# Both slots' maxima on VectorE in one go, the first slot's transposed half after them: a change of order in an attention loop

## The chip, the cores and the metric

The kernel runs on one core of one Trainium2 chip. The metric is the device time of one execution in microseconds; the time before is the median of three runs. The kernel is written in Bass with Tile, in float32 throughout.

## The reference, cut to what matters

The whole program has four layers on x of shape (2, 256, 64, 64): attention, an added position term, a bottleneck with a deformable 3x3 convolution, and a block of two deformable 3x3 convolutions with group norms. The change is in the first layer:

```python
xn = group_norm(x, gn_gamma, gn_beta)                       # 8 groups
qkv = einsum('bchw,oc->bohw', xn, w_qkv).reshape(B, 3, 4, 64, 4096)
scores = einsum('bhci,bhcj->bhij', q, k) * 64 ** -0.5        # 4096 x 4096 per image and head
attn = softmax(scores, axis=-1)
out = einsum('bhij,bhcj->bhci', attn, v).reshape(B, C, H, W)
x = xn + einsum('bchw,oc->bohw', out, w_proj) + b_proj
```

With two images and four heads there are eight attention matrices of 4096 x 4096. A softmax row needs its greatest score before the exponential.

## The kernel before, in words

The kernel has two stages. The first, `attention`, does the attention, the position term, and as background work the first part of the bottleneck (its 1x1 convolution, its offsets and, for image 0, its sampling and products). The second, `deform`, does the rest.

In `attention`, a *unit* is one image and one pair of heads; there are four. A unit is cut into 16 *blocks* of 256 query positions, and a block into 16 *slots*. A slot n is a quarter c of the keys (1024 of them), a half t of the block's queries (128) and one head h of the pair, in the order c, t, h. There are 256 slots in a unit and 1024 in all. For each slot:

- `scores(n)` (line 569): TensorE multiplies the queries with the keys, into a PSUM tile `sc` of 128 x 1024. Each of the two matrix products runs as two passes, and the two run side by side on two halves of the array's rows. The pool of `sc` has two buffers, so the products of slot n+2 can start only when the exponential of slot n has read its scores.
- `lowest(n)` (line 581): VectorE takes the greatest score of each row, negated, into a column of the tile `low`.
- `exponentials(n)` (line 587): ScalarE takes exp(score - greatest) from PSUM into a tile `e` in SBUF, with the row's sum.
- `turn(n)` (line 599): TensorE transposes `e` in 16 pieces of 64 x 64, alternating between two PSUM tiles `tt` (one for each half of the rows). The pool has two buffers in all, so `turn(n + 1)` can write its two tiles only when those of `turn(n)` have been copied away.
- `keep(n, ...)` copies the two `tt` tiles to the tile `et` in SBUF: the first on ScalarE (line 618), the second (j = 1) on VectorE (line 616). In units 2 and 3 ScalarE also takes the second one for the slots with h = 1 and t = 0.
- `attend(n)` (line 628): TensorE multiplies a part of the transposed weights of four slots with the values, into the PSUM tile `av`. After the last part VectorE copies it to `o` (line 463).

The quarters of the keys are put together later, by their maxima, in the class `Block` (`compare`, `raised`, `weights`, `spread`, `combine`).

The order of instructions on TensorE, ScalarE, VectorE and GpSimd is the order in which the program writes them: the stage runs inside `tc.manual_schedule` for these four engines, and Tile adds the semaphores. The main loop, `while n < last + 4 ...`, takes two slots a turn, n (even) and n + 1. On TensorE a turn of the loop is `scores(n + 2)`, `scores(n + 3)`, `turn(n)`, `small(n)`, `attend(n - 4)`, `attend(n - 3)`, `small(n + 1)`, `turn(n + 1)`. On VectorE it is the copy of slot n - 1, `lowest(n + 2)`, the copy of slot n, `lowest(n + 3)`, then what `small`, `attend` and `background` add. On ScalarE it is the copy of slot n - 1 and the copies put off to `ps.flush`, `exponentials(n + 2)`, the copy of slot n, what `small` adds, `exponentials(n + 3)`. `small` runs whatever falls due at a slot (queries, keys and values of what comes next, the blocks' own steps), and in units 2 and 3 a step of background work where nothing is due; `background` runs steps of the other layers' work.

Of the kernel before, what the change touches and what calls it, by code (L numbers as in the profile page):

```python
# [60 lines left out]
class Net:  # L61
# [108 lines left out]
    def attention(self, bott):  # L170
# [5 lines left out]
        with ExitStack() as ctx:  # L176
# [81 lines left out]
            def prepare(b):  # L258
                for coef in stats_of(b, (block(a["x"][b], i) for i in range(NB))):
                    yield True  # L260
                for i in range(NB):
                    normalize(b, i, coef, block(a["x"][b], i))
                    yield True
# [294 lines left out]
            def parts(n):  # L558
                u, r = divmod(n, per_unit)
                return u, r // 16, r % 16 // 4, r % 4 // 2, r % 2  # L560

            def scores(n):
                u, i, c, t, h = parts(n)
                if n % 16 == 0:
                    blocks[n // 16] = Block(u, i)
                s = psc.tile([P, 2, 512], F32, name="sc")
                at = 256 * (i % 2) + P * t
                for j in range(2):
                    nc.tensor.matmul(  # L569
                        s[:, j, :],  # L570
                        lhsT=q[u, i // 2][int(h != j)][halves[j], at : at + P],
                        rhs=k[u][c][halves[j], h, :],
                        start=True,
                        stop=True,
                    )
                return s.rearrange("p j n -> p (j n)")

            def lowest(n, s):
                u, i, c, t, h = parts(n)
                low = blocks[n // 16].low[:, 2 * t + h, c : c + 1]  # L580
                nc.vector.tensor_reduce(low, s, AX.X, ALU.max, negate=True)  # L581

            def exponentials(n, s):
                u, i, c, t, h = parts(n)
                e = ep.tile([P, 2, 512], F32, name="e")
                blk, g = blocks[n // 16], 2 * t + h
                nc.scalar.activation(  # L587
                    e.rearrange("p j n -> p (j n)"), s, AF.Exp,
                    bias=blk.low[:, g, c : c + 1], accum_out=blk.sum[:, g, c : c + 1],
                )  # L590
                return e

            def turn(e):


                out = [ptp.tile([P, 8, 64], F32, name="tt") for _ in range(2)]
                for m in range(8):
                    for half, pt in zip(halves, out):
                        nc.tensor.transpose(  # L599
                            pt[:, m, :],  # L600
                            e[half, m // 4, m % 4 * P : m % 4 * P + P],
                            self.ident[half, half],
                        )
                return out

            def keep(n, pts, engine):

                u, i, c, t, h = parts(n)
                if n % 4 == 0 and n // 4 not in ets:
                    ets[n // 4] = etp.tile([P, 8, 2, 256], F32, name="et")  # L610
                for j, pt in enumerate(pts):
                    at = P * t + 64 * j
                    dst = ets[n // 4][:, :, h, at : at + 64]
                    if j and (u < 2 or h == 0 or t):
                        if engine == "DVE":
                            nc.vector.tensor_copy(dst, pt)  # L616
                    elif engine == "ACT":
                        nc.scalar.copy(dst, pt)  # L618

            def attend(n):  # L620

                j, part = divmod(n, 4)
                u, i, c, _, _ = parts(4 * j)
                if part == 0:
                    now["av"] = pav.tile([P, 256], F32, name="av")
                for m in (2 * part, 2 * part + 1):
                    for h in range(2):
                        nc.tensor.matmul(  # L628
                            now["av"][halves[h], :],
                            lhsT=v[u][c][:, m, halves[h]],  # L630
                            rhs=ets[j][:, m, h, :],
                            start=(m == 0),
                            stop=(m == 7),
                        )
                if part == 3:
                    blocks[j // 4].product(c, now["av"])
                    del ets[j]

            def first_batch():
                yield from bott.conv(0, bt, ps)  # L640
                yield from self.early_image(bott, bt, ps)
# [7 lines left out]
            def background(count):  # L649
                for g in list(back):  # L650
                    while count:
                        r = next(g, None)
                        if r is None:
                            back.remove(g)
                            break
                        if not r:
                            break
                        count -= 1
# [5 lines left out]
            n = 0  # L664
            while n < last + 4 or back or any(own.values()):
                u, d = divmod(n, per_unit)
                if d == 0 and u < len(units):
                    plan_unit(u)
                    if u == 0:
                        back.append(prepare(1))  # L670
                    if u == 1:
                        back.append(bott.before(0, bt, ps))
                    if u == 2:
                        back.append(first_batch())
                    if u == 3:
                        back.insert(0, bott.before(1, bt, ps))

                def small(at):
                    steps = own.pop(at, ())
                    for f in steps:  # L680
                        f()
                    if not steps and u > 1:
                        background(1)

                if n - 1 in pts:
                    p = pts.pop(n - 1)
                    keep(n - 1, p, "ACT")
                    keep(n - 1, p, "DVE")
                ps.flush()
                sc = [scores(m) for m in (n + 2, n + 3) if m < last]  # L690
                if sc:
                    lowest(n + 2, sc[0])
                if n < last:
                    p = turn(e.pop(n))
                    keep(n, p, "DVE")
                if sc:
                    lowest(n + 3, sc[1])
                    e[n + 2] = exponentials(n + 2, sc[0])
                if n < last:
                    keep(n, p, "ACT")  # L700

                small(n)
                if 4 <= n < last + 4:
                    attend(n - 4)
                    attend(n - 3)
                small(n + 1)
                if n < last:
                    pts[n + 1] = turn(e.pop(n + 1))
                if sc:
                    e[n + 3] = exponentials(n + 3, sc[1])  # L710
                if u or n % 8 == 0:
                    background(1)
                n += 2
# [828 lines left out]
```

## Time and profile before

| What | Value |
|---|---|
| Median of 3 runs | 5279.05 us (5276.96 to 5280.33) |
| The profiled execution's own time | 5435.25 us |
| Its span, first to last instruction | 5433.5 us, mean granted TensorE clock 0.962 |
| Busy: PE, VectorE, ScalarE, GpSimd | 91%, 78%, 52%, 41% of the span |
| First and last score product of the loop | 58 us and about 3024 us after the start |
| Greatest score of a slot (line 581) | 1024 instructions, mean 1217 ns |
| Exponential of a slot (line 587) | 1024 instructions, mean 1114 ns |
| VectorE's copy of a transposed half (line 616) | 896 instructions, mean 688 ns |
| ScalarE's copy of a transposed half (line 618) | 1152 instructions, mean 579 ns |

The names: PE is TensorE's matrix products and transposes, PEld its weight loads, DVE is VectorE, ACT is ScalarE, POOL is GpSimd. A row of the timeline has the start and the duration in us, the engine, the line, the operation, the tile written and the tiles read, and in brackets how long the engine sat idle before it and what ended that. A line of the waits says which instruction waited for which: us in total, how often, and the longest. A line of the table by stretches has start and end, the length, each engine's busy time with its count of instructions, then the granted TensorE clock, the share of the DMA engines and GB/s. A busy PE can hide short pauses, because matrix products overlap each other in the record and their ends are modelled.

### The profile page before, as it was taken

What the parts mean: (1) busy time and instruction counts of PE and PEld (TensorE: products, weight loads), DVE (VectorE), ACT (ScalarE), POOL (GpSimd) and SP (SyncE); (2) the same over time, 40 slices, a digit from 0 to 9 for tenths busy, and PEclk for the clock granted to TensorE, in tenths of its full rate; (3) what the DMA queues carried; (4) which work ended last, traced back from release to release, by engine and by line L of the source; (5) the groups of instructions that cost most, each with busy time, mean ns of one, the idle gap of its engine ahead of it and who ended that gap; (6) DMA issues with size and microseconds to landing.
All of it is one profiled execution on the core that took longest, in us unless ns stands there. A gap on an engine that the chain in (4) does not pass through costs nothing. (4 is left out here: it accounts for less than half of the span.)

```text
span 5433.5 us, 99236 instructions
## 1 busy us (share of the span) xinstructions
PE 4919.1 (91%) x37976; PEld 2646.2 (49%) x37976; DVE 4241.2 (78%) x7922; ACT 2847.4 (52%) x5189; POOL 2241.7 (41%) x2241
## 2 busy tenths in 40 slices
PE   8999999999999999999999656556999999999998
PEld 5555565555555555555555322222444444444443
DVE  6878868787677878677777466667989999999998
ACT  5676656666566666566666222122444444444443
POOL 0111110000026666462000366665556566666565
PEclk9999999999999999999999877778999999999999
DMA  5221121111122333233311466556989999999998
GB/s 167 63 86 60 40 69 33 48 33 40 60 62 84 94 91 97 91 90 90 98 27 34 137 196 193 190 193 201 372 316 324 341 357 349 341 389 344 337 345 296
DMA packets 347147, 920.40 MB, mean 169 GB/s; under 512 B 58716, under 2 KB 98458, under 8 KB 346670
## 3 DMA queue, kind: packets, MB, share of 16 engines
q0 software_dynamic: 194688, 683.85, 35.8%
q1 hardware_dynamic: 151982, 230.20, 13.5%
q8 instruction: 298, 4.88, 0.4%
q14 instruction: 179, 1.47, 0.1%
HBM read 815.90 MB, written 89.60 MB: 167 GB/s over the span
## 5 line engine op out<-in xcount | busy, mean ns | idle before, releaser
L1312 DVE SCALAR_TENSOR_TENSOR smp<-four,dw,smp 128x256 f32<-128x256 f32 x3456 | 1611.7, 483 | 253.0 <-ACT smp L1306 113.5
L587 ACT ACTIVATE e<-sc,low 128x1024 f32<-128x1024 f32 x1024 | 1140.6, 1114 | 833.5 <-DVE low L581 802.8
L818 POOL DMA_INDIRECT four<-img,didx x1152 | 1153.4, 1001 | 728.0 <-DVE smp L1312 337.7
L581 DVE TENSOR_REDUCE low<-sc 128x1 f32<-128x1024 f32 x1024 | 1246.4, 1217 | 219.1 <-PE sc L569 213.8
L1343 PE MATMUL out<-st,wc 128*128 128x512 f32 x2304 | 1242.4, 622 | 125.0 <-ACT st L1333 60.2
L569 PE MATMUL sc<-k,qs 64*128 64x512 f32 x2048 | 1025.2, 616 | 5.0 <-ACT e L587 3.9
L569 PE MATMUL sc<-k,q 64*128 64x512 f32 x2048 | 1007.9, 616 | 0.0
L628 PE MATMUL av<-et,v 128*64 128x256 f32 x8192 | 1007.0, 386 | 0.0
L508 POOL TENSOR_TENSOR o<-o,f 128x1024 f32<-128x1024 f32 x64 | 151.6, 2369 | 1912.8 <-DVE o L463 950.7
L599 PEld LDWEIGHTS tt<-ident,e 64*128 64x128 f32 x16384 | 654.5, 139 | 542.5 <-ACT et L618 253.3
L616 DVE COPY et<-tt 128x512 f32<-128x512 f32 x896 | 616.4, 688 | 254.1 <-PE tt L599 221.1
L599 PE MATMUL tt<-ident,e 64*128 64x64 f32 x16384 | 733.5, 226 | 58.9 <-ACT et L618 33.5
L1333 ACT COPY st<-pt 128x1024 f32<-128x1024 f32 x288 | 291.1, 1011 | 896.5 <-PE pt L1324 637.6
L618 ACT COPY et<-tt 128x512 f32<-128x512 f32 x1152 | 653.0, 579 | 130.0 <-PE tt L599 119.4
L628 PEld LDWEIGHTS av<-et,v 128*64 128x64 f32 x8192 | 557.7, 137 | 308.7 <-issue 59.8
L1324 PEld LDWEIGHTS pt<-ident,smp 128*128 128x128 f32 x2304 | 320.9, 145 | 793.9 <-issue 514.6
L818 POOL DMA_INDIRECT bfour<-img,bidx x576 | 579.8, 1007 | 270.1 <-issue 113.7
L1343 PEld LDWEIGHTS out<-st,wc 128*128 128x128 f32 x2304 | 394.1, 197 | 386.7 <-issue 272.2
L1324 PE MATMUL pt<-ident,smp 128*128 128x128 f32 x2304 | 461.2, 283 | 107.9 <-DVE smp L1312 77.3
L1306 ACT ACTIVATE smp<-four,dw 128x256 f32<-128x256 f32 x1152 | 512.4, 502 | 87.7 <-DMA four<-img,didx 68.4
L778 PE MATMUL pd<-x,wf 128*126 128x512 f32 (+2 forms) x896 | 459.0, 598 | 11.1 <-DMA x<-xn 9.9
L569 PEld LDWEIGHTS sc<-k,qs 64*128 64x128 f32 x2048 | 328.1, 188 | 272.0 <-ACT e L587 199.0
(160 smaller groups left out, 3365.0 us busy)
## 6 DMA issues: line engine op xcount, KB each, us to landing
f<-share_d SPq DMA_DIRECT2D x128, 256.0 KB
xb<-xn SPq DMA_DIRECT2D x55, 512.0 KB
img<-imgt SPq DMA_DIRECT2D x96, 256.0 KB
four<-img,didx POOLq DMA_INDIRECT x1152
xa<-res SPq DMA_DIRECT2D x32, 512.0 KB
xb<-in_x SPq DMA_DIRECT2D x20, 512.0 KB
bfour<-img,bidx POOLq DMA_INDIRECT x576
qs<-q SPq DMA_DIRECT2D x64, 128.0 KB
```

The costliest lines, as they stand in the source:

```text
L569: nc.tensor.matmul(s[:, j, :], lhsT=q[u, i // 2][int(h != j)][halves[j], at : at + P], rhs=k[u][c][halves[j], h, :], start=True, stop=True,)
L581: nc.vector.tensor_reduce(low, s, AX.X, ALU.max, negate=True)
L587: nc.scalar.activation(e.rearrange("p j n -> p (j n)"), s, AF.Exp, bias=blk.low[:, g, c : c + 1], accum_out=blk.sum[:, g, c : c + 1],)
L599: nc.tensor.transpose(pt[:, m, :], e[half, m // 4, m % 4 * P : m % 4 * P + P], self.ident[half, half],)
L616: nc.vector.tensor_copy(dst, pt)
L618: nc.scalar.copy(dst, pt)
L628: nc.tensor.matmul(now["av"][halves[h], :], lhsT=v[u][c][:, m, halves[h]], rhs=ets[j][:, m, h, :], start=(m == 0), stop=(m == 7),)
L818: self.nc.gpsimd.indirect_dma_start(out=dst, out_offset=None, in_=img, in_offset=bass.IndirectOffsetOnAxis(ap=idx, axis=0),)
L1306: nc.scalar.mul(smps[s], fours[s][:, 0], weight(s, 0))
L1312: nc.vector.scalar_tensor_tensor(smps[s], four[:, c], weight(s, c), smps[s], ALU.mult, ALU.add)
L1324: nc.tensor.transpose(pts[u][:, c, j * P : (j + 1) * P], smp[:, c * P : c * P + P], self.ident,)
L1343: nc.tensor.matmul(outs[ob], lhsT=wc[k][:, c, ob * P : ob * P + P], rhs=sts[u][:, c, :], start=(k == 0 and c == 0), stop=(k == K2 - 1 and ...
```

## The change

Within a turn of the loop, `lowest(n + 3)` moves from behind `keep(n, p, "DVE")` to directly behind `lowest(n + 2)`. On VectorE the order copy of n - 1, maximum of n + 2, copy of n, maximum of n + 3 becomes copy of n - 1, maximum of n + 2, maximum of n + 3, copy of n. No instruction is added or removed, and the program's order on the other engines is the same. `keep(n, p, "DVE")` issues one copy for every even slot, so one maximum and one copy change places in each of 511 turns (the first two slots are begun ahead of the loop, and the last turn has no new scores).

```diff
                 sc = [scores(m) for m in (n + 2, n + 3) if m < last]
-                if sc:
-                    lowest(n + 2, sc[0])
+                for m in range(len(sc)):
+                    lowest(n + 2 + m, sc[m])
                 if n < last:
                     p = turn(e.pop(n))
                     keep(n, p, "DVE")
                 if sc:
-                    lowest(n + 3, sc[1])
                     e[n + 2] = exponentials(n + 2, sc[0])
                 if n < last:
                     keep(n, p, "ACT")
```

## The prediction

> **What bounds the kernel now.** I read the page first for the shares, then the busy time by stretches, then the waits, then the timeline of one iteration. The page and the table of stretches (start:end, length, then busy time of PE, PEld, DVE, ACT, POOL):
>
> ```profile
> PE 4919.1 (91%) x37976; PEld 2646.2 (49%) x37976; DVE 4241.2 (78%) x7922; ACT 2847.4 (52%) x5189; POOL 2241.7 (41%) x2241
> 58.00:1462.00 1404.00, 1386.27 (x15245) 805.04 (x15245) 1085.07 (x1544) 919.03 (x1661) 153.61 (x101) 1.00 0.18 56
> 1462.00:3040.00 1578.00, 1509.58 (x15677) 876.08 (x15675) 1170.60 (x1706) 1018.60 (x1854) 627.02 (x682) 0.99 0.26 76
> ```
>
> The changed loop runs from 58 to 3040 us. PE is busy 99% and 96% there; VectorE is at 77% and 74%. So TensorE is the bound of this stage, and only time that PE loses can be won. The "busy" figure hides short losses, because a matmul row overlaps its neighbours. So I looked at who PE's weight loads waited for (total us, times, longest):
>
> ```profile
> ACT e L587 <- DVE low L581: 802.8, 860, 6.2
> PEld tt L599 <- ACT et L618: 253.3, 696, 6.2
> DVE et L616 <- PE tt L599: 221.1, 461, 6.6
> PEld sc L569 <- ACT e L587: 199.0, 327, 2.3
> ```
>
> ScalarE's exponential waits for the maximum 860 times of 1024. VectorE's copy waits for the transposes 461 times. And 327 score products find their PSUM buffer still held by an exponential. One iteration (start, duration) shows the links:
>
> ```profile
> 1003.12 0.65 PE L569 MATMUL sc<-k,qs 64*128 64x512 f32 x1
> 1004.06 0.18 PEld L569 LDWEIGHTS sc<-k,qs 64*128 64x128 f32 x1 [0.69 <-ACT e L587]
> 1004.27 1.22 DVE L581 TENSOR_REDUCE low<-sc 128x1 f32<-128x1024 f32 x1
> 1004.59 0.59 PE L569 MATMUL sc<-k,qs 64*128 64x512 f32 x1
> 1005.02 0.66 PE L599 MATMUL tt<-ident,e 64*128 64x64 f32 x16
> 1005.59 1.11 ACT L587 ACTIVATE e<-sc,low 128x1024 f32<-128x1024 f32 x1 [1.11 <-DVE low L581]
> 1005.75 0.69 DVE L616 COPY et<-tt 128x512 f32<-128x512 f32 x1 [0.25 <-PE tt L599]
> 1006.35 1.22 DVE L581 TENSOR_REDUCE low<-sc 128x1 f32<-128x1024 f32 x1
> 1006.70 0.58 ACT L618 COPY et<-tt 128x512 f32<-128x512 f32 x1
> 1007.49 0.71 PE L599 MATMUL tt<-ident,e 64*128 64x64 f32 x16
> 1007.66 1.11 ACT L587 ACTIVATE e<-sc,low 128x1024 f32<-128x1024 f32 x1 [0.27 <-DVE low L581]
> 1008.92 0.18 PEld L569 LDWEIGHTS sc<-k,qs 64*128 64x128 f32 x1 [0.63 <-ACT e L587]
> ```
>
> In it the second slot's maximum (1006.35) starts only after the first slot's copy, which waited for the transposes. Its exponential runs 1007.66 to 1008.77. The next iteration's second score product, which reuses that buffer, loads weights at 1008.92, 0.15 us later: just released, with nothing prepared.
>
> **What this costs today.** I tallied the 508 full iterations from the same timeline. A score product is two passes. With the exponential long done (0.4 us or more before the product) the two passes start 0.429 us apart. If the exponential ended under 0.15 us before (113 iterations), they start 0.533 apart and the product itself begins 0.093 late; at 0.15 to 0.18 (97 iterations) 0.502 apart. The sum over the 284 iterations with under 0.4 us is 20.5 us between passes and 11.0 us of late starts: 31.5 us. Check: among iterations with nothing else in PE's queue, the 147 tight ones last 4.87 us, the 56 loose ones 4.81, mostly 4.79.
>
> **What the Trainium skill says.** "PSUM — Partial Sum Buffer", Engine vs sequencer instructions: the VectorE and ScalarE queues are strict FIFO. The trace agrees: the second maximum stands behind a copy that idled 0.25 us, though its scores were there. "TensorE: Matmul & The Clock Gate", What happens when you issue a matmul: weight loads are pulled ahead of running matmuls, matmuls stay in order. The trace agrees: 0.43 us between passes where the load could go early, 0.53 where it could not. "PSUM — Partial Sum Buffer", Specifications: ScalarE and VectorE read PSUM in parallel at full rate if the banks differ. The maximum takes 1.202 to 1.226 us in all 1024 rows, whichever reader runs beside it, so I leave its duration alone when it moves beside an exponential.
>
> **The change part by part.** No instruction is added or removed, on any queue; no DMA moves, and SP's and POOL's queues are not touched. One VectorE maximum (1.217 us mean) goes ahead of one VectorE copy (0.688 us), 512 times. PE's and ScalarE's own order stays.
>
> *Second maximum, earlier.* Count from the iteration's first score product at 0. The first maximum runs 1.13 to 2.35. The second slot's scores are ready by about 1.99 (last pass at 1.35, and 0.64 as between pass and maximum elsewhere). Neighbouring VectorE rows overlap by 0.09, so the second maximum runs 2.26 to 3.47; before it ran from 3.1 or 3.2 to about 4.4. It ends 0.8 or more earlier. Its exponential cannot use all of that: it stands behind ScalarE's copy, which ends at 4.16. So it starts near 4.15 and not at 4.54; from the rows of all iterations, 0.37 to 0.52 us earlier (median 0.48) in units 0 and 1, 0.43 median in units 2 and 3. A spare of 0.15 becomes 0.5 to 0.6, in the class where the passes are 0.429 apart. **Gain up to 31.5 us, on PE's path.**
>
> *Copy, later.* It now follows the second maximum: 3.38 to 4.07, against 2.63 to 3.32. Who waits for it: the transposes of the second slot, which reuse its PSUM tile, at 4.24 to 4.37. The spare between copy and those transposes was 1.06 us (median, units 0 and 1). After the move, with 0.06 for the release, it is 0.23 (tenth percentile 0.10; units 2 and 3: 0.27 and 0.06), and above zero in all 507 iterations that I worked through. The reason is that ScalarE's copy of the other half, on which the same transposes wait, ends 0.05 us later still: the chain maximum, exponential, copy on ScalarE is as long as maximum, maximum, copy on VectorE. **Cost 0**, hidden by ScalarE's copy. If that cover went, the transposes would wait for VectorE.
>
> *VectorE's wait for the transposes goes.* It sat idle about 0.3 us there; now the second maximum fills it, so what follows (the copy of av, corner arithmetic, the mixing of samples) starts some 0.35 us earlier. Where VectorE runs without a gap until the next copy or maximum, this reaches PE: the transposes' second half waits 33.9 us in 50 places, of which 4.2 us would go; their first half, through the exponential, 19.0 us in 58 places, of which 6.0 would go. The rest wait for products of PE or other engines and stay. **Gain 0 to 10.2 us**; half of it, 5, is taken, since these stalls share iterations with the first.
>
> *Sum.* 31.5 less a fifth, for waits that show up next once PE runs closer to ScalarE (the spare before the odd transposes shrinks from 0.24 to about 0.1), is 25; plus 5 is **30 us**. The profiled execution took 5435.25 us (span 5433.5), so its successor would take about 5405. The median of the runs is 5279.05, 156 us less; I take the same 30 us off, since the loss sits in a PE-bound stage at a clock of 0.99 to 1.00: **5249 us**. Bounds: all of both gains, 42 us, gives 5237; none, 5279.
>
> **The rivals.**
> *Faster, as above*: 0.70. For it: the loose iterations exist in this very trace and last 4.79 us.
> *The wait changes owner (no change)*: PE reaches the odd transposes 0.1 us earlier and finds ScalarE's copy, or VectorE's, not done. ScalarE's loop is transposes, scores, maximum, exponential, copy, transposes: about 0.05 + 0.55 + 4.13 = 4.73 us. PE's own floor is 4.79. Against: 0.06 of room; for: units 2 and 3 have more in the queues. Left over would be 5 to 8 us: about 5272. Chance 0.14, with the case that the order makes no difference.
> *VectorE becomes the link (slower)*: the copy's spare of 0.23 us is gone if two maxima back to back do not overlap as a copy and a maximum do (0.09 each), or if the second pays for a wait of its own on the products. No row of before has two long maxima in a row, so this is bounded: from 0 to some 0.4 us later per iteration. At 0.4 the odd transposes wait 0.17 us in the 284 tight iterations, 48 us, against 31 won: 5296. It decides from 0.34 us on (0.23 of spare and 31.5/284 = 0.11 of gain). Chance 0.16.
>
> **How the numbers follow.** About 0.2% (10.6 us) is what a measurement can tell from no change. Faster 0.70, within 0.14, slower 0.16. The range takes both gains in full and 7 us more where later waits shrink too (5230), and reaches through no change to a slight loss (5283); the slower rival is left out. For the likeliest case alone: 5237 to 5265.
>
> **What would show it.** After: VectorE's rows go maximum, maximum, copy, the second maximum starting 1.12 us after the first; "PEld sc <- ACT e" falls from 199 us and 327 times to under a third; "DVE et <- PE tt" falls by about half; the passes of the second score product stand 0.43 us apart; plain iterations last 4.79 to 4.82 us; the attention stage shortens by 25 to 35 us and the rest keeps its length. Wrong, if the two maxima start 1.25 us or more apart, if "PE tt <- DVE et" grows from 22 us to over 60, or if a gain sits outside 58 to 3040 us.

## The result, and the profile after

The changed kernel takes 5241.25 us (median of 6 runs, 5236.85 to 5243.06), the kernel before 5278.01 us in the same comparison (6 runs). The ratio is 0.9931, 95% interval 0.9921 to 0.9941: 36.8 us less. The forecast was 5249 us.

The head of the page after, and its table by stretches, cut at the first and last product of the attention loop (columns as before):

```profile
PE 4868.1 (93%) x37976; PEld 2657.6 (51%) x37976; DVE 4207.5 (80%) x7922; ACT 2815.3 (54%) x5189; POOL 2246.8 (43%) x2241
57.00:1452.00 1395.00, 1380.33 (x15354) 820.29 (x15355) 1066.41 (x1554) 901.67 (x1670) 153.64 (x101) 1.00 0.18 56
1452.00:2982.00 1530.00, 1480.24 (x15565) 875.54 (x15561) 1152.62 (x1696) 991.67 (x1846) 628.60 (x680) 0.99 0.27 78
```

The counts of instructions are the same; the loop now ends at 2982 us and not at 3039. But this profiled execution took 5241.94 us, and the first one of before 5435.25 us. So their difference is not the change's alone: against that trace the loop is 56 us shorter and what lies behind it 137 us. A second profile of before, which took 5283.75 us, gives the fair comparison (first experiment).

The waits of the loop after (total us, times, longest):

```profile
ACT e L587 <- DVE low L581: 780.4, 494, 6.3
PEld tt L599 <- ACT et L618: 178.1, 411, 5.8
DVE et L616 <- PE tt L599: 155.9, 200, 5.1
PEld sc L569 <- ACT e L587: 86.2, 307, 1.9
```

ScalarE's exponential waits for a maximum far less often (494 times, not 860): the second one of a turn now finds it ready. VectorE's copy waits for transposes 200 times, not 461. The last line has nearly as many waits as before, 307 against 327, and needs the timeline to be read rightly. The same turn as in the prediction:

```profile
988.24 1.13 ACT L587 ACTIVATE e<-sc,low 128x1024 f32<-128x1024 f32 x1
989.00 0.65 PE L569 MATMUL sc<-k,q 64*128 64x512 f32 x1
989.51 0.18 PEld L569 LDWEIGHTS sc<-k,qs 64*128 64x128 f32 x1 [0.26 <-ACT e L587]
989.92 0.59 PE L569 MATMUL sc<-k,q 64*128 64x512 f32 x1
990.16 2.35 DVE L581 TENSOR_REDUCE low<-sc 128x1 f32<-128x1024 f32 x2 [0.23 <-PE sc L569]
990.35 0.59 PE L569 MATMUL sc<-k,qs 64*128 64x512 f32 x1
990.77 0.66 PE L599 MATMUL tt<-ident,e 64*128 64x64 f32 x16
991.48 1.11 ACT L587 ACTIVATE e<-sc,low 128x1024 f32<-128x1024 f32 x1 [1.54 <-DVE low L581]
992.43 0.68 DVE L616 COPY et<-tt 128x512 f32<-128x512 f32 x1
992.58 0.57 ACT L618 COPY et<-tt 128x512 f32<-128x512 f32 x1
993.16 1.11 ACT L587 ACTIVATE e<-sc,low 128x1024 f32<-128x1024 f32 x1
993.24 0.71 PE L599 MATMUL tt<-ident,e 64*128 64x64 f32 x16
993.79 0.65 PE L569 MATMUL sc<-k,q 64*128 64x512 f32 x1
```

The two maxima stand in one row of 2.35 us, so they start 1.13 us apart. The exponential of the odd slot (993.16) follows ScalarE's copy at once. The exponential that holds the buffer of the odd score product ends at 989.37. The product's weights load at 989.51, still on its heels, but 0.41 us ahead of the product at 989.92, which has 0.55 us of spare: the wait remains in the list and has left the path. Before the change, load and product both started 0.15 us after the exponential. The passes (989.92, 990.35) are 0.43 us apart, and the turn lasts 4.79 us where it lasted 4.92.

### The profile page after: what moved, and what is told of

Same layout as the page of the kernel before. It is cut to its first block, busy times and chain, and to the rows that moved or that the text cites. A ratio compares the mean times of both kernels' runs of the same rounds, so it can differ in the third digit from the quotient of the medians.

```text
span 5240.2 us, 99232 instructions
## 1 busy us (share of the span) xinstructions
PE 4868.1 (93%) x37976; PEld 2657.6 (51%) x37976; DVE 4207.5 (80%) x7922; ACT 2815.3 (54%) x5189; POOL 2246.8 (43%) x2241
## 3 DMA queue, kind: packets, MB, share of 16 engines
q0 software_dynamic: 194688, 683.85, 36.8%
## 4 chain that ended last, share of the span: by engine, by line
PE 65%; DVE 16%; DMA 6%; issue 6%; ACT 5%; POOL 3%; SPq 0%; ACTq 0%; DVEq 0%; POOLq 0%
PE av L628 15%; PE sc L569 14%; PE out L1342 10%; PE tt L599 9%; DVE smp L1311 8%; PE pd L777 5%; DMA four<-img,didx 4%; PE pt L1323 3%; POOL bfour L817 2%; DVE low L581 2%; ACT e L587 2%; PE pm L1039 1%; PE pm L271 1%; PE pm L533 1%; DMA bfour<-img,bidx 1%
## 5 line engine op out<-in xcount | busy, mean ns | idle before, releaser
L581 DVE TENSOR_REDUCE low<-sc 128x1 f32<-128x1024 f32 x1024 | 1204.2, 1217 | 236.6 <-PE sc L569 234.0
L569 PE MATMUL sc<-k,qs 64*128 64x512 f32 x2048 | 998.4, 606 | 0.6 <-ACT e L587 0.3
L569 PE MATMUL sc<-k,q 64*128 64x512 f32 x2048 | 979.8, 605 | 0.0
L1305 ACT ACTIVATE smp<-four,dw 128x256 f32<-128x256 f32 x1152 | 523.3, 503 | 460.4 <-DMA four<-img,didx 392.2
L599 PE MATMUL tt<-ident,e 64*128 64x64 f32 x16384 | 726.5, 226 | 47.1 <-DVE et L616 22.3
L569 PEld LDWEIGHTS sc<-k,qs 64*128 64x128 f32 x2048 | 346.1, 188 | 215.1 <-issue 118.1
```

Of the source, the lines that this page charges most:

```text
L569: nc.tensor.matmul(s[:, j, :], lhsT=q[u, i // 2][int(h != j)][halves[j], at : at + P], rhs=k[u][c][halves[j], h, :], start=True, stop=True,)
L599: nc.tensor.transpose(pt[:, m, :], e[half, m // 4, m % 4 * P : m % 4 * P + P], self.ident[half, half],)
```

## The experiments

Two quantities are taken from every trace in the same way. The *loop* is the time from its first score product to its last product with the values. The *start of the odd exponential* is its start less the end of ScalarE's copy of slot n (median, units 0 and 1): 0.39 us before, -0.11 after. Four of the kernels below (act_pad256, act_pad448 and the two dve_pad) ran on another chip than the rest of the experiments, and there the kernel before takes 5483.54 us. The traces put that difference mostly behind the loop (2438 to 2449 us there, 2256 to 2264 in the traces of the first chip), and the first profile of before, which was long behind the loop in the same way (2395 us), has units 0 and 1 as long as the second (1412.8 and 1412.7 us). So across the two chips I compare ratios, and the length of units 0 and 1.

**The kernel before, again.**

> The kernel before, unchanged, profiled once more. Its first profile ran 5435 us while its runs had a median of 5279 us, so the difference of the two traces (56 us in the attention loop, 137 us after it) is larger than the measured 37 us. Theory: the attention loop alone carries the gain, so a profile that runs near 5279 us has a loop about 37 us longer than after (2961 us against 2925), about 18 us of it in units 0 and 1, and the same length behind the loop. Rival (a part of the gain lies behind the loop): the stretch behind the loop is over 10 us longer than after's 2258 us, and the loop less than 27 us longer.

One run, 5283.75 us. The loop is 2960.2 us, after 2924.6: 35.6 us less, 18.1 in units 0 and 1 and 17.5 in units 2 and 3. Behind the loop it is 2264.1 against 2258.6; this execution lasted 6 us longer than the kernel's median. So the loop carries the gain. Its waits, to be set beside those of the first profile and of after:

```profile
PEld tt L599 <- ACT et L618: 241.7, 691, 5.9
DVE et L616 <- PE tt L599: 198.8, 430, 6.3
PEld sc L569 <- ACT e L587: 190.1, 322, 2.3
```

**The new order in half of the units.**

```diff
+                early = u < 2          # u01_only; u > 1 in u23_only
-                for m in range(len(sc)):
+                for m in range(len(sc) if early else min(1, len(sc))):
                     lowest(n + 2 + m, sc[m])
...
                     keep(n, p, "DVE")
+                if sc and not early:
+                    lowest(n + 3, sc[1])
```

> The new order in units 0 and 1 only, the old one in units 2 and 3. Theory (the buffer of the scores is released in time): in units 0 and 1 the tally gave 14.5 us of late and slow score products and 0.6 us of stalls behind VectorE, and the two traces differ by 18.2 us there, so the gain is 15 to 18 us of the 37: about 5262 us. Rival (the gain comes from VectorE's freed idle time, which matters where background work keeps it busy, in units 2 and 3): a gain under 5 us here.

5256.23 us against 5276.47, ratio 0.9964 (0.9951 to 0.9978): 20.2 us, a little over the 15 to 18 expected, which lie within the interval.

> The new order in units 2 and 3 only. Theory: 16.9 us of late and slow score products plus up to 10 us of stalls behind VectorE, so a gain of 17 to 24 us: about 5257 us. Rival (VectorE's freed idle time is the gain): 32 us or more here. The two gains should add up to after's 37 us if nothing couples the units.

5261.14 us, ratio 0.9971 (0.9960 to 0.9981): 15.3 us. That is a little under the 17 to 24 expected, and the interval reaches to 21. The two add up to 35.6 us, and units 0 and 1, where the first tally had only 0.6 us of stalls behind VectorE, give about half. That speaks against the rival that lives on VectorE being held up by background work, as far as these units go. The intervals do not say which half gives more.

**The odd exponential held back.** VectorE keeps the new order; ScalarE copies part of a constant onto itself ahead of the odd exponential. This undoes the early exponential, and with it what follows on ScalarE, at the price of more work there. act_pad224 has the first of the two copies alone, the longer pads have both.

```diff
                     keep(n, p, "ACT")
+                    nc.scalar.copy(self.shift[:, :7, :], self.shift[:, :7, :])   # act_pad224: 224 columns
+                    nc.scalar.copy(self.shift[:, :1, :], self.shift[:, :1, :])   # and this: 32 in act_pad256, [:, :7] in act_pad448
```

> The new order, and ScalarE copies 224 columns of a constant onto itself (about 0.47 us a row, some 0.38 us of ScalarE's time) between its copy of slot n and the exponential of slot n+3. The exponential of the odd slot then starts about as late as in the kernel before, while VectorE keeps its new order. Theory (release of the score buffer): the spare before the odd score product falls from 0.55 us to about 0.17, the passes are 0.50 apart again in some 250 iterations, and 20 to 32 us of the 37 are lost: about 5266 us. Rival (VectorE's earlier finish is the gain): at most 5 us are lost, about 5244 us.

5248.93 us, ratio 0.9949 (0.9935 to 0.9962). About a quarter of the gain went (0.9949 against 0.9931): both figures in the expectation missed. The pad had moved the exponential less than I had meant, to 0.17 us, and left 0.34 us of spare before the odd product (median, units 0 and 1), where the passes stand 0.429 us apart. It was too short to decide, and longer ones follow.

> The new order with two copies on ScalarE before the exponential of slot n+3, one of 224 columns and one of 32. The single copy of 224 moved that exponential by 0.28 us and left a spare of 0.34 us, where the tally shows no slow pass. The second one should add 0.12 us: spare about 0.16, as in the kernel before. Theory (the score buffer's release is the gain): passes 0.50 apart in some 230 iterations, 18 to 27 us lost against after, so 5259 to 5268. Rival (what the first pad cost, about 8 us, is ScalarE's load and grows with the load): 0.12/0.28 of 8 more, about 5252.

5478.01 us against 5483.54, ratio 0.9997 (0.9987 to 1.0007). **The whole gain is gone**, 36 us and not 18 to 27, with the exponential at 0.43 us, where it had been before (0.39). A turn of it:

```profile
1006.77 0.68 DVE L616 COPY et<-tt 128x512 f32<-128x512 f32 x1
1006.86 0.58 ACT L618 COPY et<-tt 128x512 f32<-128x512 f32 x1
1007.33 0.39 ACT L700 COPY shift<-shift 128x224 f32<-128x224 f32 x1
1007.75 0.22 ACT L701 COPY shift<-shift 128x32 f32<-128x32 f32 x1
1007.99 1.10 ACT L587 ACTIVATE e<-sc,low 128x1024 f32<-128x1024 f32 x1
1009.23 0.18 PEld L569 LDWEIGHTS sc<-k,qs 64*128 64x128 f32 x1 [0.83 <-ACT e L587]
1009.23 0.69 PE L569 MATMUL sc<-k,qs 64*128 64x512 f32 x1
1009.76 0.59 PE L569 MATMUL sc<-k,qs 64*128 64x512 f32 x1
```

VectorE's copy is in its new place. The odd score product (1009.23) starts with its own weight load, 0.14 us after the exponential's end at 1009.09, and its second pass follows 0.53 us later: the picture of before.

> The same with two copies of 224 columns: the exponential of slot n+3 moves by 0.56 us and would end about when the odd score product wants to start. Theory: the product then starts 0.15 us after the exponential's end and with slow passes, so about 0.24 us is lost in each of some 230 tight iterations: 55 us against after, about 5296, slower than before. Rival (load): 16 us against after, about 5257.

5511.41 us, ratio 1.0063 (1.0046 to 1.0079): slower than before, and by more than expected: 35 us by the ratio, where 55 against after less the 37 won made 18. Put together, units 0 and 1. The last column is the part of the one before it that lies in the odd score products: how much later they start after the even ones, and how much farther apart their passes are, summed over the full turns.

| Kernel | Start of the odd exponential, us | Units 0 and 1, us | Longer than after, us | In the odd products, us |
|---|---|---|---|---|
| after | -0.11 | 1394.6 | 0 | 0 |
| act_pad224 | 0.17 | 1395.8 | 1.2 | 0.9 |
| before | 0.39 | 1412.8 | 18.2 | 14.9 |
| act_pad256 | 0.43 | 1414.9 | 20.3 | 18.1 |
| act_pad448 | 0.60 | 1431.8 | 37.2 | 32.7 |

The first 0.28 us cost 1.2 us, the next 0.26 us cost 19.1. A load of ScalarE that cost time as such would not be expected to jump like this; the cost has a threshold, the kernel before, without a pad, lies on the same curve, and most of it stands in the products that wait for the release of the score buffer. In units 0 and 1 these products are 15 of the 18 us that the change won. In units 2 and 3 the same sum, from the second profile of before, gives 9.2 of 17.5 us.

**The copy held back.** This is the slower rival's place: one more VectorE instruction ahead of the copy of slot n, in the new order and in the old.

```diff
                     p = turn(e.pop(n))
+                    nc.vector.tensor_max(self.shift, self.shift, self.shift)
                     keep(n, p, "DVE")
```

> The new order, and VectorE takes the maximum of a 128x224 constant with itself (a row of about 0.39 us, some 0.29 us of VectorE's time) between the second maximum and its copy of slot n. Theory (in the new order the copy is nearly the last thing the odd transposes wait for; its spare is 0.16 us with 0.06 for the release, so 0.10): some 0.19 us is lost in each of about 230 tight iterations, 44 us, and a little where VectorE is late: about 5287. Rival (the copy still has room): under 8 us lost, about 5247.

> The same instruction in the same place ahead of the copy of slot n, in the kernel before. There VectorE sat idle 0.25 to 0.3 us at this place, waiting for the transposes. Theory: nearly free; the second maximum moves by under 0.05 us, so the odd product's spare of 0.15 shrinks by that: 0 to 12 us lost against before, 5278 to 5290. Rival (VectorE's load itself costs): as much as in the new order, some 44 us, about 5322.

Ratios 1.0130 (1.0110 to 1.0150) and 1.0103 (1.0084 to 1.0122): 2.0% lost after the change (against its 0.9931), and 1.0% before it. Both are well over what I expected (44 us, and at most 12), and the pair decides nothing, because the pad itself was not steady. Its row in the new order (min/median/max in ns):

```profile
L695 DVE TENSOR_TENSOR shift<-shift x512: 368/382/2652, 67.6 to 3091.6; 128x224 f32<-128x224 f32 x171
```

57 of the 512 took over 0.5 us, 46 us above the median in all; in the old order 61 and 47 us. GpSimd's longest tensor operations of this stretch (line 508) take 2.37 us. The Trainium skill ("SBUF — State Buffer", Who interferes with whom) says that a VectorE instruction with two SBUF inputs contends with a GpSimd instruction that reads SBUF, and that on this chip a reduction never does. The traces agree: every one of the 57 and 61 lies beside a GpSimd instruction. So the next pad was a reduction of the same 224 columns.

```diff
+                    nc.vector.tensor_reduce(
+                        self.shift[:, 6, 31:32], self.shift.rearrange("p t o -> p (t o)"),
+                        AX.X, ALU.min,
+                    )
                     keep(n, p, "DVE")
```

> The new order with a cleaner pad between the second maximum and the copy of slot n: VectorE reduces a 128x224 constant in SBUF to a column (one input; the earlier pad with two inputs was held up behind GpSimd 57 to 61 times of 512, 46 us in all). About 0.29 us of VectorE's time. Theory (the copy is the link with 0.10 us of room): about 0.19 us in each turn whose odd transposes are not held up by other work, which the first pad showed to be most of them: 70 to 95 us lost against after, ratio to before 1.006 to 1.012. Rival (room left): ratio under 0.996.

> The same pad in the kernel before, in the idle time ahead of the copy of slot n. Theory: nearly free without GpSimd in the way, since VectorE waited 0.25 to 0.3 us there: 0 to 15 us, ratio 1.000 to 1.003. Rival (VectorE's load costs as such, or late turns carry it): about as much as with the first pad, ratio 1.008 or more.

The row is steady now:

```profile
L695 DVE TENSOR_REDUCE shift<-shift x512: 364/376/387, 68.8 to 3029.7; 128x1 f32<-128x224 f32 x171
```

After the change the pad gives a ratio of 1.0037 (1.0023 to 1.0051), 56 us over after's ratio, under the 70 to 95 expected; before it 1.0029 (1.0017 to 1.0040), 15 us, at the top of what was expected. In the new order the gap between the first and second transpose of an odd turn, which is the wait for VectorE's copy, grows by 55 us over the loop (from 6.7 to 61.8 us); the loop grows by 56.7. In the old order it grows by 0.4. A turn of the new order with the pad:

```profile
1009.41 0.65 PE L569 MATMUL sc<-k,q 64*128 64x512 f32 x1
1012.86 0.38 DVE L695 TENSOR_REDUCE shift<-shift 128x1 f32<-128x224 f32 x1
1013.01 0.57 ACT L618 COPY et<-tt 128x512 f32<-128x512 f32 x1
1013.15 0.68 DVE L616 COPY et<-tt 128x512 f32<-128x512 f32 x1
1013.71 0.89 PE L599 MATMUL tt<-ident,e 64*128 64x64 f32 x16
```

The copy ends at 1013.83, 4.42 us into the turn; the transposes began at 4.30, and their row is 0.89 us long, not 0.71. The median gap is 0.18 us. The pad takes 0.29 us from the next instruction (1012.86 to 1013.15); less the 0.10 us of room that makes 0.19. So the slower rival named the right link, and what spared the change is 0.10 us of room.

**ScalarE's copy ahead of the even exponential.**

```diff
+                if n < last:
+                    keep(n, p, "ACT")
                 if sc:
                     e[n + 2] = exponentials(n + 2, sc[0])
-                if n < last:
-                    keep(n, p, "ACT")
```

> The new order, and on ScalarE the copy of slot n goes ahead of the exponential of slot n+2. The transposes of slot n are done at about 2.2 us of the turn and the first maximum ends at 2.35, so the copy ends near 2.75 and not 4.16, and the exponentials run 2.75 to 3.86 and 3.86 to 4.97. Theory: the odd transposes then wait for VectorE's copy alone, which ends 0.05 us before ScalarE's did, so the 13 us of stalls behind ScalarE's copy shrink by some 2 to 8 us only: ratio to before 0.9915 to 0.993. Rival (ScalarE's copy was the link): the 13 us go, ratio 0.9905 or less.

> The same swap on ScalarE in the kernel before. There VectorE's copy of slot n is 1 us ahead of the odd transposes, so ScalarE's copy alone holds them. Theory: the 14.6 us of stalls behind it go nearly whole (8 to 14 us, ratio 0.9973 to 0.9985), while the late exponential of slot n+3 stays, because it waits for VectorE's second maximum and not for ScalarE's order. Rival (the late exponential is due to ScalarE's queue): the odd score products come in time too and 25 us or more go, ratio 0.995 or less.

On the new order: 5239.24 us against 5277.89, ratio 0.9929 (0.9916 to 0.9943), not to be told from after's 0.9931. The stalls of the odd transposes behind ScalarE's copy, 13.4 us in after's trace, are gone; some 11 us of stalls behind VectorE's copy stand in their place. On the old order: ratio 0.9985 (0.9979 to 0.9992), 8 us faster. There the stalls go without a successor, and the late odd exponential stays: its trace has 33 us of late and slow odd products, more than the 24 us without the swap. It waits for VectorE's maximum, not for ScalarE's order. No version tried is measurably faster than the changed kernel.

## Why the prediction was right, step by step

*The bound.* Right. 35.6 us of the gain lie in the PE-bound loop, and they came from PE's short losses under a busy share of 96 to 99%.

*The odd score product, 31.5 us.* The mechanism is shown: held back, the exponential takes the whole gain with it, and the loss stands in the odd products. The size was off. The tally of after leaves 1 to 2 us of it, so nearly all of what there was went. But there was less: the second profile of before has 24.1 us of late and slow products, not 31.5. The first profile was 20 us longer in units 2 and 3 and had 9.2 us of late starts there, the second 2.7. I had set the excess of 156 us of that execution aside and yet took the tally from it.

*The copy at no cost.* Right, by little. The median spare of the odd transposes behind it is 0.16 us after, 0.10 with the release (I had 0.23). In the turn above the copy ends at 4.11 us and not at 4.07, and the transposes come at 4.24, the early end of what I had. PE's transposes waited 22.3 us for the copy in the loop after, 22.4 and 21.5 in the two profiles of before.

*VectorE's freed time, 5 of 10.2 us.* Not shown. 35.6 less about 24 us in the odd products leaves some 12 us in the loop, more than the 5 taken, but not where I had put them. The stalls of the odd transposes behind ScalarE's copy fell from 14.6 to 13.4 us only. From the odd transposes to the next score product there are some 4 us less, from the last pass of the scores to the second transpose of an even turn 2.3 us less; the rest is spread. In units 0 and 1 only 3 us lie outside the odd products, and act_pad256 gives most of them back, so there they hang on the exponential as well. In units 2 and 3, where the background work is, it is some 8 us, and act_pad256 ran on another chip. Whether VectorE's earlier finish has a share in these stays open.

*The sum.* That 30 us came near to 36.8 is in part luck. The discount of a fifth, for waits that show up next, was not needed: after it stood 25 us, about what the odd products gave, only because the tally had been a third too large. And the 5 us of the other term stand against 12 that it does not account for.

*The markers.* Right: maxima 1.13 to 1.14 us apart, passes 0.43, plain turns 4.79 (and one maximum and one copy change places 511 times, not 512). The 35.6 us out of the loop are just over the 25 to 35 forecast. Wrong: "PEld sc <- ACT e" was to fall under a third and fell to 86 us and 307 times, because a weight load may wait where the product does not (0.41 us ahead of it in the turn above); and "DVE et <- PE tt" fell by a fifth to a third in time, by half only in count.

*The rivals.* "The wait changes owner" did not come: the stalls of the odd transposes behind ScalarE's copy did not grow. "VectorE becomes the link" is refuted as the outcome and confirmed as the next limit. The sign named for it, "PE tt <- DVE et" over 60 us, would have missed it: dve_red_after lost some 55 us to that very copy, and the list has 22.8 us there, since its record counts PE as busy in nearly all of these gaps. They show only between the starts of the two transposes.

## What to carry to other kernels

In a loop bound by one engine, ask of each buffer not only whether it is free in time for the instruction that reuses it, but whether it is free early enough for that instruction's preparation: here a spare under 0.15 us cost 0.10 us between the passes in each such turn, and 0.34 us cost next to nothing. When two instructions on a helper engine change places, follow both to the instruction that needs them and compare the spares; the one that gives way may end within a tenth of a microsecond of being the new limit. And take a tally of small losses from a profile whose execution lasts as long as the timed runs.

## What the runs showed of the hardware that was not expected

A VectorE instruction with two SBUF inputs that has a median of 0.38 us was held up to 2.65 us beside GpSimd instructions, in 11% of its executions; the reduction with one input never took more than 0.39 us. The two differ in their operation and in the size of what they write as well. And the kernel before lasted 5278 us in one comparison and 5484 in another, on another chip. Its two profiled executions, of 5284 and 5435 us, show where a difference of that kind lies: units 0 and 1 of the attention agree within 0.1 us, units 2 and 3 differ by 20 us, and the stretch behind the loop, where the DMA engines' mean share was 0.91 in the first profile from 3650 us on, differs by 131 us. Why it does is not shown.
